# A four-layer image network on one core: one more product on GpSimd, another order of the last image's scans, and bias work on VectorE at the end

## The chip, the core and the metric

The kernel runs on one core of a Trainium2 chip. The core has TensorE (PE in the profile), VectorE (DVE), ScalarE (ACT), GpSimd (POOL) and SyncE (SP, which here issues every DMA). The metric is the device time of one execution in microseconds; the kernel before was run three times.

## What is computed

Four images of 96 channels and 64 x 64 pixels pass through four layers. What matters here is the first, a selective scan in four directions, and the feed-forward blocks of the last two, which round to 8-bit and 16-bit floats:

```python
# layer 0: K, N, DI = 4 orders, 16 states, 192 channels; L = 4096 pixels
xs = jnp.stack([xf, xt, jnp.flip(xf, -1), jnp.flip(xt, -1)], axis=1)   # rows, columns, and both backwards
...
dA = jnp.exp(dt_[..., None] * A[None])
hst = hst * dA + (dt_ * ut)[..., None] * bt[:, :, None, :]
y = jnp.einsum('bkdn,bkn->bkd', hst, ct)
...
y = y0 + y1 + y2 + y3            # orders 1 and 3 turned back to rows
# then a norm over channels, a product with Wout, and the residual

def _qlinear(x, W, b):           # in the feed-forwards of layers 2 and 3
    y = q_acc(jnp.einsum('bsk,nk->bsn', q_mul(x), q_mul(W)))
    return q_acc(y + q_mul(b))
h = jax.nn.relu(_qlinear(x, W1, b1))
y = _qlinear(h, W2, b2)
```

Layer 1 is an expansion to 576 channels, a 3 x 3 depthwise convolution and a projection; layer 2 starts with a Fourier transform over the pixels, layer 3 with a linear attention. Each has its own residual.

## The kernel before

**The scan is the backbone.** `scans` builds a list of 128 *steps*: for each image, for each order k in `KORDER` = (0, 1, 3, 2), for each of 8 chunks of 512 pixels. Orders 0 and 2 go over rows, 1 and 3 over columns; 2 and 3 run backwards, so their chunks come from 7 down to 0. A step has 12 *units*, one for each pair of 32-channel groups and quarter of the states: units 0 to 7 are the first pass (128 channels), 8 to 11 the second (64). A loop over *slots* writes the program out by hand, one unit a slot, each engine's part at its own offset:

- ScalarE, one slot ahead (`decays`): first `keep`, which saves the last column of an earlier unit as the start of the next chunk, then two exponentials of 128 x 512 into PSUM (line 1188).
- GpSimd, two slots ahead (`inputs`): db = g * B, one product of 128 x 1024 (line 1178).
- VectorE (`states`): two scans of 128 x 512 (line 1197), and for most units two products with C (line 1201).
- For units whose number is in `POOL_C` = (1, 3, 6, 8, 10), GpSimd multiplies with C instead, a slot later (`product`, line 1216, 128 x 1024), and also saves the last columns (line 1213; otherwise ScalarE does, line 1211).
- TensorE adds the states of two units into a PSUM tile (`sums`, line 1237), two slots after the later one. After the last pair of a pass ScalarE copies the tile out (line 1245) and two stores of y are put down with `later`.

g, the step widths and B, C are tiles broadcast from DRAM. `LOADS` says at which unit a tile of the next step is loaded: B and C of state quarter 0 at unit 4, quarter 1 at unit 10, quarter 2 at unit 11, quarter 3 at unit 0 of the step itself. Five buffers hold the B, C tiles (rep_BC), three the others. `later` only notes a store; `flush`, the first thing in a slot, issues what was noted. All loads and stores stand in SP's one queue.

**The work beside.** Everything else is written as Python generators that yield the engine, a guessed cost and the PSUM banks of their next piece. In each slot `advance` takes pieces from the first *stage* in a list while the slot's room lasts. `SHARE` gives an engine's room: (us added per slot, most that is kept), 3.0 and 3.2 for TensorE, 2.4 and 3.0 for ScalarE, 1.2 and 1.7 for VectorE. The stages in order: weights, `front` of images 1 and 2 (input convolution and the scans' inputs), for image 0 the turn, layer 1 with the scan's output stage (`conv_block`), layers 2 and 3, then `front` of image 3, and images 1 and 2 likewise. The layer 1 stage of the last image comes at the end of the list.

**The turn** (`turn`) adds orders 1 and 3, turned by strided reads, to order 0 and the skip term, in two parts: channels 0 to 127 (lo = 0) and the other 64 (lo = 128). A part loads 2 x 2 MB of y (lines 636 to 638 are its matmuls). It waits until three orders of its image are scanned (`scanned[b] < 3 * NCH`); those of images 2 and 3 stand in one stage with layer 3 of the image before. `scan_outputs` then adds order 2, chunk by chunk (line 677), as soon as its last order has passed a chunk, and the output norm follows (lines 696 to 713).

**The tail.** After the last slot, what is left is issued by `force`, without regard to slots, and with all eight PSUM banks (`alone` is not empty then): the rest of layer 1 of image 3 (lines 763, 786, 802, 803, and 839, 845 of its norms), the two halves of the Fourier layer, layer 2's end and layer 3, three chunks at a time. In `feed_forward` each of three 128-row parts of the hidden layer takes three passes of ScalarE: a copy from PSUM to 16 bits (line 868), bias and relu (line 871), rounding to 8 bits (line 873).

Of the kernel before, what the change touches and what calls it, by code (L numbers as in the profile page):

```python
# [37 lines left out]
NI, NJ = DI // 32, NS // 4  # L38
ROWB = 256

KORDER = (0, 1, 3, 2)

SCAN = {"rep_d": 3, "rep_g": 3, "rep_BC": 5, "db": 3, "hc": 5}
POOL_C = (1, 3, 6, 8, 10)
TMP, IN = 10, 5

PC = NI * NJ // 2
# [4 lines left out]
WORK = {"weights": 47.0, "turn": 70.0, "front": 417.0, "conv": 447.0,  # L52
        "spectral": 111.2, "layer_2": 231.0, "product": 1.2, "layer_3": 153.6, "layer_3_turn": 223.6}
RATE = 6.0
SHARE = {"pe": (3.0, 3.2), "act": (2.4, 3.0), "dve": (1.2, 1.7)}
NQ, NG, NPAIR = 4, HID // 32, H // 2


# [35 lines left out]
def hybrid_kernel(ctx: ExitStack, tc: tile.TileContext, a: dict):  # L94
# [45 lines left out]
    def const(name, rows=slice(0, 128)):  # L140
        return cst[rows, CS[name]]
# [282 lines left out]

    to_store = []

    def later(out, t):

        to_store.append((out, t))

    def flush():
        while to_store:
            store(*to_store.pop(0))

    def ahead(n, first, items):

# [3 lines left out]
                got.append(first(items[len(got)]))  # L440
            yield item, got[i]

    def in_turn(items, make, matmuls, take, evict, depth=2):

        made = []

        def oldest():
            p, item, at = made.pop(0)
            yield take[:3] + (at,)
            evict(p, item)  # L450
            free()

        for n, item in enumerate(items):
            yield make[:3] + (n > 0,)
            p = bank()
            matmuls(p, item)
            made.append((p, item, clock[0]))
            if len(made) == depth:
                yield from oldest()
        while made:  # L460
            yield from oldest()
# [147 lines left out]

    def turn(b):  # L610

        im = b % 2
        while scanned[b] < 3 * NCH:
            yield wait(1)
        parts = [big("ya"), big("yb")]
        for lo in (0, 128):
            for t, k in zip(parts, (1, 3)):
                load(t[:, :L].rearrange("p (c l) -> p c l", c=NCH),
                     d_y[k][im][:, lo : lo + 128, :].rearrange("c p l -> p c l"))

            def fetch(c):
                y, u = (t[:, L + c % 4 * CH : L + c % 4 * CH + CH] for t in parts)
                load(y, d_y[0][im][c, lo : lo + 128])
                load(u[: min(128, DI - lo)], d_skip[b][c, lo : min(lo + 128, DI)])
                return y, u

            whole = lo == 0
            m, add = (128, const("ident")) if whole else (64, const("two")[:, :64])
            skip = skips[:, 0] if whole else skips[:64, 1, :64]

            def added(p, of):
                c, (y, u) = of
# [4 lines left out]
                mm(p, lhsT=add, rhs=y, start=False, stop=False)  # L637
# [10 lines left out]
            yield from in_turn(chain([first], chunks), pe(3.8, 1), added, ac(0.6), stored)  # L648
            yield wait(2)

    def scan_outputs(b, done):

        there = lambda c: scanned[b] >= 4 * NCH - c

        def fetch(c):
            out = []
            for of in (d_yt[b % 2][c], d_y[2][b % 2][c]):
                for part in (of[:128], of[128:]):
                    s = arrival("ypart")
                    load(s[: part.shape[0]], part)  # L660
                    out.append(s[: part.shape[0]])
            return out[0], out[2], out[1], out[3]

        coming = None
        for c in reversed(range(NCH)):
            while not there(c):
                yield wait(1)
            if coming is None:
                coming = fetch(c)
                yield wait(3)  # L670
            parts, coming = coming, None
            y = []
            for name, of in (("ident", parts[:2]), ("two", parts[2:])):
                yield pe(1.8, 1, name == "two")
                p = bank()
                for n, s in enumerate(of):
                    mm(p, lhsT=const(name, slice(0, s.shape[0])), rhs=s, start=n == 0, stop=n == 1)  # L677
# [178 lines left out]
    def feed_forward(x, weights):  # L856

        wq1, wq2, bq = weights
        xq = tmp("xq", (128, CH), F8)
        yield from layer_norm(x[:C], xq)  # L860
        hq = tmp("hq", (128, 3, CH), F8)
        for m in range(3):
            yield pe(0.5, 1, m > 0)
            p = bank()
            mm(p, lhsT=wq1[:, m * 128 : (m + 1) * 128], rhs=xq, start=True, stop=True)
            yield ac(0.65)
            acc = tmp("acc16", (128, CH), F16)
# [252 lines left out]
    def scans(stages):  # L1120
# [6 lines left out]

        steps = []
        for b in range(B):
            for k in KORDER:  # L1130
# [95 lines left out]
        def sums(group):  # L1226
# [6 lines left out]
            for m in (1, 0):  # L1233
                x = group[m]
                for e in (1, 0):
                    q = 2 * m + e
                    done = mm(y[32 * q : 32 * q + 32], lhsT=const("stack"), rhs=x["hc"][:, e],  # L1237
                              start=first or (x["pass"] == 0 and x["j"] == 0), stop=last or (x["pass"] == 0 and x["j"] == NJ - 1))
                    if made is None:
                        made = group[0]["made"]  # L1240
                        tc.add_manual_dep(done.ins, made.ins.name, mybir.DependencyInfo(
                            mybir.DependencyClass.Sync, mybir.DependencyReason.DATA), reason="sums")
            if last:
# [299 lines left out]
```

## Time and profile before

| | us |
|---|---|
| three runs | 6702.1, 6703.26, 6710.55 (median 6703.26) |
| the profiled execution | 6708.94 |
| its span, first to last instruction | 6707.1 |
| first scan starts, last scan ends (line 1197) | 78.8, 6125.9 |
| layer 1 of image 3, last block ends | 6323 |
| the Fourier layer ends | 6472 |
| layer 2 ends, layer 3 begins | 6605 |

| engine | busy us | share | instructions |
|---|---|---|---|
| TensorE, matmuls | 4836.7 | 72% | 27884 |
| VectorE | 5521.4 | 82% | 5803 |
| ScalarE | 4357.4 | 65% | 8296 |
| GpSimd | 5173.5 | 77% | 2743 |

The profile's page gives busy times, the span in 40 slices, the chain of work that ended last, and the costliest groups of instructions: line, engine, operation, output<-inputs, shape, count | busy us, mean ns of one | idle time of the engine just before them and what ended most of it. The trace also answers for a stretch of time: busy time of each engine in it, the clock that TensorE was granted, and the share of the DMA engines' time. A float32 matmul of the program is two records. Busy times of neighbouring instructions can overlap by some tens of ns, so that sums of means lie a little above busy time.

### The profile page before, as it was taken

Reading aid. Unit: us, or ns where it says so; the run is one execution under the profiler, and the core shown is the slowest. Engines: PE = TensorE matmul, PEld = TensorE weight load, DVE = VectorE, ACT = ScalarE, POOL = GpSimd, SP = SyncE. Lnnn points to the kernel's source line nnn. Section 1 sums busy time; section 2 is a strip of 40 time slices with the busy share of each in tenths; the row PEclk is TensorE's granted clock in tenths of the full one; section 3 lists DMA queues with packets and bytes.
Section 4 is the critical chain, followed back from the end, with each engine's and each line's share of the span. In section 5 each row is a group of like instructions: output and inputs, shape, how many; then the busy total and the mean of one; then the engine's idle time right before and its main releaser. Section 6 shows DMA issues by size and latency. Waiting matters only on the chain. (4 is left out here: it accounts for less than half of the span.)

```text
span 6707.1 us, 84452 instructions
## 1 busy us (share of the span) xinstructions
PE 4836.7 (72%) x27884; PEld 1777.4 (26%) x27884; DVE 5521.4 (82%) x5803; ACT 4357.4 (65%) x8296; POOL 5173.5 (77%) x2743
## 2 busy tenths in 40 slices
PE   7633857657987676775688777777887776779986
PEld 2100212111223531121122254221223532213562
DVE  5979899898999889889999988887999889895110
ACT  5743767765665577876556656866665677755367
POOL 4756878789999789977999988888999889894000
PEclk9755968768998787797799988878998887889997
DMA  5644555576644544455765454465644544563120
GB/s 185 193 157 142 180 188 188 180 239 231 188 152 143 181 154 145 156 187 187 257 208 165 147 168 167 144 208 176 193 151 151 193 157 145 202 230 101 38 82 27
DMA packets 438825, 1121.42 MB, mean 167 GB/s; under 512 B 73002, under 2 KB 74768, under 8 KB 437140
## 3 DMA queue, kind: packets, MB, share of 16 engines
q1 hardware_dynamic: 438388, 1116.02, 50.9%
q8 instruction: 222, 3.64, 0.2%
q14 instruction: 215, 1.76, 0.1%
HBM read 881.28 MB, written 239.01 MB: 167 GB/s over the span
## 5 line engine op out<-in xcount | busy, mean ns | idle before, releaser
L1178 POOL TENSOR_TENSOR db<-rep_g,rep_BC 128x1024 f32<-128x1024 f32 x1536 | 3600.2, 2364 | 551.0 <-DMA rep_BC<-bc 281.9
L1188 ACT ACTIVATE ps_da<-rep_d,aneg 128x512 f32<-128x512 f32 x3072 | 2067.3, 690 | 542.0 <-DVE hc L1197 404.5
L1197 DVE TENSOR_TENSOR_SCAN ps_da<-ps_da,state,db 128x512 f32<-128x512 f32 x1568 | 2007.1, 1280 | 237.3 <-ACT state L1211 154.5
L1216 POOL TENSOR_TENSOR hc<-hc,rep_BC 128x1024 f32<-128x1024 f32 x640 | 1510.8, 2361 | 91.0 <-DVE hc L1197 41.4
L1237 PE MATMUL ps_y<-hc,cst 128*32 128x512 f32 x6144 | 1026.7, 746 | 619.3 <-POOL hc L1216 348.2
L1197 DVE TENSOR_TENSOR_SCAN hc<-ps_da,state,db 128x512 f32<-128x512 f32 x1120 | 1371.1, 1266 | 70.3 <-ACT ps_da L1188 23.1
L1201 DVE TENSOR_TENSOR hc<-ps_da,rep_BC 128x512 f32<-128x512 f32 x1792 | 1239.2, 692 | 112.5 <-PE ps_y L1237 3.9
L1211 ACT COPY state<-ps_da 128x1 f32<-128x1 f32 x1568 | 247.2, 158 | 471.1 <-DVE hc L1201 466.3
L1237 PEld LDWEIGHTS ps_y<-hc,cst 128*32 128x32 f32 x6144 | 145.8, 119 | 1264.8 <-POOL hc L1216 556.6
L786 PE MATMUL ps_mm<-h,wd 128*32 128x512 f32 x3048 | 348.5, 593 | 7.0 <-ACT r L153 7.0
L1213 POOL COPY state<-hc 128x2 f32<-128x2 f32 x560 | 106.0, 189 | 306.9 <-DVE hc L1197 294.2
L531 PE MATMUL ps_mm<-xp,taps 128*128 128x512 f32 x576 | 293.6, 652 | 41.5 <-ACT xp L511 14.4
L1197 DVE TENSOR_TENSOR_SCAN ps_da<-ps_da,db 128x512 f32<-128x512 f32 x224 | 273.6, 1221 | 41.7 <-ACT state L1211 23.8
L582 PE MATMUL ps_mm<-xd,dtw 128*128 128x512 f32 x256 | 177.1, 783 | 162.2 <-ACT z L604 116.2
L763 PE MATMUL ps_mm<-wd,w 128*32 128x512 f32 x2032 | 261.2, 621 | 36.8 <-DMA wd<-x 11.9
L1245 ACT COPY yt<-ps_y 128x512 f32<-128x512 f32 x256 | 149.1, 582 | 151.1 <-PE ps_y L1237 145.1
L591 ACT ACTIVATE z<-ps_mm 128x512 f32<-128x512 f32 x192 | 114.3, 595 | 167.8 <-PE ps_mm L582 106.6
L912 PE MATMUL ps_mm<-wa,xp 128*64 128x96 f32 x1728 | 143.2, 327 | 103.1 <-DVE d L916 79.1
L597 DVE SCALAR_TENSOR_TENSOR ps_mm<-ps_mm,z 128x512 f32<-128x512 f32 x192 | 132.3, 689 | 99.1 <-ACT z L595 69.6
L1197 DVE TENSOR_TENSOR_SCAN hc<-ps_da,db 128x512 f32<-128x512 f32 x160 | 186.2, 1204 | 9.4 <-ACT ps_da L1188 9.0
L845 PE MATMUL ps_mm<-r,cst 128*128 128x512 f32 x206 | 138.8, 761 | 70.8 <-ACT acc L868 26.6
L569 PE MATMUL ps_mm<-ua,sel 128*128 128x512 f32 x128 | 101.3, 880 | 114.7 <-ACT z L604 91.1
(420 smaller groups left out, 6954.1 us busy)
## 6 DMA issues: line engine op xcount, KB each, us to landing
rep_BC<-bc SPq DMA_DIRECT2D x512, 512.0 KB
rep_g<-du SPq DMA_DIRECT2D x384, 512.0 KB
rep_d<-delta SPq DMA_DIRECT2D x384, 512.0 KB
y<-yt SPq DMA_DIRECT2D x512, 128.0 KB
du<-g SPq DMA_DIRECT2D x128, 256.0 KB
delta<-z SPq DMA_DIRECT2D x128, 256.0 KB
tab<-in_etab SPq DMA_DIRECT2D x128, 256.0 KB
du<-g SPq DMA_DIRECT2D x128, 128.0 KB
```

Of the source, the lines that this page charges most:

```text
L531: mm(p, lhsT=taps[:, t, 0:128], rhs=window(t, c + e), start=t == 0, stop=t == 8)
L582: mm(p, lhsT=dtw[:, o + 2 * part, 0:128], rhs=xd, start=True, stop=True)
L763: mm(p[32 * n : 32 * n + 32], lhsT=w1[:, 32 * g : 32 * g + 32], rhs=xin[:, n : n + 15 : 2, 1 : W + 1], start=True, stop=True)
L786: mm(p[32 * n : 32 * n + 32], lhsT=held["wd"][:, groups[i], o, dx, :], rhs=here[i][:, :, dx : dx + W], start=dx == 0, stop=dx == 2)
L1178: nc.gpsimd.tensor_mul(x["db"], x["step"]["g"][x["i"]], both(x["step"]["BC"][x["j"]][:, 0]))
L1188: act(x["da"][e], x["step"]["d"][x["i"]][:, e], AF.Exp, scale=aneg[:, av : av + 1])
L1197: nc.vector.tensor_tensor_scan(x["h"][e][:, order], x["da"][e][:, order], x["db"][:, e, order], start, ALU.mult, ALU.add)
L1201: x["made"] = nc.vector.tensor_mul(x["hc"][:, e], x["h"][e], x["step"]["BC"][x["j"]][:, 1])
L1211: nc.scalar.copy(to[:, e : e + 1], x["h"][e][:, end : end + 1])
L1216: x["made"] = nc.gpsimd.tensor_mul(x["hc"], x["hc"], both(x["step"]["BC"][x["j"]][:, 1]))
L1237: done = mm(y[32 * q : 32 * q + 32], lhsT=const("stack"), rhs=x["hc"][:, e], start=first or (x["pass"] == 0 and x["j"] == 0), stop=last or ...
L1245: nc.scalar.copy(yt, y)
```

## The change

Three things change, and some numbers of the planner with them.

1. `POOL_C` becomes (1, 3, 5, 7, 9, 11): six of twelve units have their C product on GpSimd, every second one. `SHARE` becomes 2.4 and 2.8 for ScalarE and 1.5 and 2.0 for VectorE.
2. The last image's orders are scanned as 1, 3, 0, 2. Its turn may start when two orders are through; the part with lo = 128 comes first and leaves y0 out, the part with lo = 0 takes y0's chunks as order 0's scan delivers them (`ready`). `scan_outputs` of the last image loads y0's upper rows as a fifth piece and adds them there. The turn goes over its chunks upwards instead of downwards, for all images. `scanned` counts a chunk when its second store is issued, no longer when it is noted. `flush` moves behind the slot's loads of B, C, g and step widths.
3. When nothing but the tail is left (`alone`), `feed_forward` does bias and relu on VectorE, and for the middle of the three parts the rounding to 8 bits too.

```diff
-KORDER = (0, 1, 3, 2)
+KORDER = [(0, 1, 3, 2)] * (B - 1) + [(1, 3, 0, 2)]
-POOL_C = (1, 3, 6, 8, 10)
+POOL_C = (1, 3, 5, 7, 9, 11)
-SHARE = {"pe": (3.0, 3.2), "act": (2.4, 3.0), "dve": (1.2, 1.7)}
+SHARE = {"pe": (3.0, 3.2), "act": (2.4, 2.8), "dve": (1.5, 2.0)}
...
     def flush():
         while to_store:
-            store(*to_store.pop(0))
+            out, t, then = to_store.pop(0)
+            store(out, t)
+            if then is not None:
+                then()
...
-        for n, item in enumerate(items):
+        items, n = iter(items), 0
+        while True:
+            while ready is not None and not ready(n):
+                yield wait(1)
+            item = next(items, None)
+            if item is None:
+                break
             yield make[:3] + (n > 0,)
...
-        while scanned[b] < 3 * NCH:
+        early = b == B - 1
+        while scanned[b] < (2 if early else 3) * NCH:
             yield wait(1)
-        for lo in (0, 128):
+        for lo in (128, 0) if early else (0, 128):
+            rows = not (early and lo == 128)
...
-                load(y, d_y[0][im][c, lo : lo + 128])
+                if rows:
+                    load(y, d_y[0][im][c, lo : lo + 128])
...
-            chunks = ahead(1, fetch, reversed(range(NCH)))
-            first = next(chunks)
+            chunks = ahead(1, fetch, range(NCH))
+            ready = (lambda n: scanned[b] >= 2 * NCH + min(n + 2, NCH)) if early and rows else (lambda n: True)
...
+            yt, y0, y2 = (of[b % 2][c] for of in (d_yt, d_y[0], d_y[2]))
+            for part in (yt[:128], y2[:128], yt[128:], y2[128:]) + ((y0[128:],) if b == B - 1 else ()):
...
-            yield ac(0.65)
-            act(acc, acc, AF.Relu, bias=bq[:, m : m + 1])
-            yield ac(0.65)
-            nc.scalar.activation(hq[:, m, :], acc, AF.Copy, saturate=False)
+            if alone:
+                yield dv(0.75)
+                nc.vector.tensor_scalar(acc, acc, bq[:, m : m + 1], 0.0, ALU.add, ALU.max)
+            else:
+                yield ac(0.65)
+                act(acc, acc, AF.Relu, bias=bq[:, m : m + 1])
+            if alone and m == 1:
+                yield dv(0.75)
+                nc.vector.tensor_copy(hq[:, m, :], acc, saturate=False)
+            else:
+                yield ac(0.65)
+                nc.scalar.activation(hq[:, m, :], acc, AF.Copy, saturate=False)
...
-                    later(to[at : at + 64].rearrange("(p e) l -> e p l", e=2), yt[64 * m : 64 * m + 64])
-                if group[0]["pass"] == 1:
-                    scanned[step["b"]] += 1
+                    later(to[at : at + 64].rearrange("(p e) l -> e p l", e=2), yt[64 * m : 64 * m + 64],
+                          through if group[0]["pass"] == 1 and m == 1 else None)
...
-            flush()
             if x is not None:
                 if x["u"] == 0:
...
                     fetch(steps[x["number"] + 1], LOADS[x["u"]])
+            flush()
             if slot + 1 < len(units):
                 decays(units[slot + 1], units[slot - 1] if slot > 0 else None)
```

More of the change, by code (lines that the diff above doesn't have):

```diff
@@ L425, in hybrid_kernel, with later @@
     to_store = []
-    def later(out, t):
-        to_store.append((out, t))
+    def later(out, t, then=None):
+        to_store.append((out, t, then))
     def flush():
         while to_store:
-            store(*to_store.pop(0))
+            out, t, then = to_store.pop(0)
+            store(out, t)
+            if then is not None:
+                then()
     def ahead(n, first, items):
@@ L441, in ahead, with in_turn @@
             yield item, got[i]
-    def in_turn(items, make, matmuls, take, evict, depth=2):
+    def in_turn(items, make, matmuls, take, evict, depth=2, ready=None):
         made = []
@@ L457, in in_turn @@
             made.append((p, item, clock[0]))
+            n += 1
             if len(made) == depth:
@@ L636, in added @@
                     mm(split(p), lhsT=add, rhs=rhs, start=n == 0, stop=False)
-                mm(p, lhsT=add, rhs=y, start=False, stop=False)
+                if rows:
+                    mm(p, lhsT=add, rhs=y, start=False, stop=False)
                 mm(p, lhsT=skip, rhs=u[: skip.shape[0]], start=False, stop=True)
@@ L643, in stored @@
                 later(d_yt[im][of[0]][lo : lo + m], s)
-            chunks = ahead(1, fetch, reversed(range(NCH)))
-            first = next(chunks)
+            chunks = ahead(1, fetch, range(NCH))
+            ready = (lambda n: scanned[b] >= 2 * NCH + min(n + 2, NCH)) if early and rows else (lambda n: True)
             yield wait(10)
-            yield from in_turn(chain([first], chunks), pe(3.8, 1), added, ac(0.6), stored)
+            yield from in_turn(chunks, pe(3.8, 1), added, ac(0.6), stored, ready=ready)
             yield wait(2)
@@ L656, in fetch @@
             out = []
[L657 to L662, printed above, removed]
+            yt, y0, y2 = (of[b % 2][c] for of in (d_yt, d_y[0], d_y[2]))
+            for part in (yt[:128], y2[:128], yt[128:], y2[128:]) + ((y0[128:],) if b == B - 1 else ()):
+                s = arrival("ypart")
+                load(s[: part.shape[0]], part)
+                out.append(s[: part.shape[0]])
+            return out
         coming = None
@@ L676, in scan_outputs @@
                 for n, s in enumerate(of):
-                    mm(p, lhsT=const(name, slice(0, s.shape[0])), rhs=s, start=n == 0, stop=n == 1)
+                    mm(p, lhsT=const(name, slice(0, s.shape[0])), rhs=s, start=n == 0, stop=n == len(of) - 1)
                 yield ac(0.6)
@@ L1129, in scans @@
         for b in range(B):
-            for k in KORDER:
+            for k in KORDER[b]:
                 for n in range(NCH):
@@ L1242, in sums, with through @@
                             mybir.DependencyClass.Sync, mybir.DependencyReason.DATA), reason="sums")
+            def through():
+                scanned[step["b"]] += 1
             if last:
```

## The prediction

> **What bounds the kernel now.** I read the page's engine line first, then the costliest groups.
>
> ```profile
> PE 4836.7 (72%) x27884; PEld 1777.4 (26%) x27884; DVE 5521.4 (82%) x5803; ACT 4357.4 (65%) x8296; POOL 5173.5 (77%) x2743
> ...
> L1178 POOL TENSOR_TENSOR db<-rep_g,rep_BC 128x1024 f32<-128x1024 f32 x1536 | 3600.2, 2364 | 551.0 <-DMA rep_BC<-bc 281.9
> ...
> L1201 DVE TENSOR_TENSOR hc<-ps_da,rep_BC 128x512 f32<-128x512 f32 x1792 | 1239.2, 692 | 112.5 <-PE ps_y L1237 3.9
> ...
> L1213 POOL COPY state<-hc 128x2 f32<-128x2 f32 x560 | 106.0, 189 | 306.9 <-DVE hc L1197 294.2
> ```
>
> Nothing is full on average, so the average decides nothing. The instructions of the scan (line 1197) run from 78.8 to 6125.9 us; behind them lies a tail of 581 us without GpSimd. I cut the scan part at every 24th scan into its 128 steps (one chunk of one order of one image; mean 47.2 us) and took busy time by windows. These are four windows of typical steps (3 to 5; 46 to 49; 100 to 103; the turn of image 2, steps 90 to 93), then the turn of image 3 (120 to 123), then the four parts of the tail. Columns: stretch, length, busy PE, PEld, DVE, ACT, POOL, clock, DMA.
>
> ```profile
> 236.70:398.80 162.10, 94.08 (x248) 20.18 (x252) 156.68 (x169) 118.21 (x236) 121.93 (x66) 0.70 0.62 197
> 2382.30:2571.20 188.90, 131.78 (x497) 44.99 (x498) 161.77 (x171) 146.93 (x281) 162.02 (x85) 0.81 0.46 151
> 4887.50:5052.10 164.60, 141.18 (x994) 38.90 (x994) 159.29 (x166) 110.70 (x217) 161.62 (x84) 0.94 0.45 153
> 4413.80:4632.10 218.30, 171.48 (x438) 43.56 (x439) 159.37 (x161) 140.27 (x281) 164.48 (x90) 0.87 0.59 193
> 5777.60:5954.60 177.00, 136.38 (x356) 30.89 (x356) 154.66 (x157) 105.04 (x216) 162.53 (x89) 0.85 0.69 241
> ...
> 6125.00:6323.00 198.00, 189.48 (x1264) 70.45 (x1256) 14.08 (x26) 72.32 (x113) 0.00 (x0) 0.98 0.12 33
> 6323.00:6472.00 149.00, 136.70 (x2565) 133.41 (x2565) 29.52 (x38) 81.36 (x99) 0.00 (x0) 0.95 0.33 102
> 6472.00:6605.00 133.00, 96.61 (x341) 42.18 (x341) 12.13 (x22) 92.82 (x165) 0.00 (x0) 0.83 0.12 36
> 6605.00:6707.00 102.00, 65.44 (x175) 24.86 (x171) 6.58 (x13) 73.84 (x131) 0.00 (x0) 0.79 0.07 22
> ```
>
> The reader is to see three kinds of step. Steps 3 to 5: VectorE 97%, GpSimd 75%. Steps 46 to 49: both at 86%, ScalarE with much work beside. Steps 100 to 103: VectorE 97% and GpSimd 98%, both at the limit. In the tail, TensorE is 96% busy in the rest of the convolution, and ScalarE 70% and 72% in the two last parts. Last, GpSimd's waits (the releaser, us in total, times, longest):
>
> ```profile
> POOL state L1213 <- DVE hc L1197: 294.2, 202, 38.8
> POOL db L1178 <- DMA rep_BC<-bc: 281.9, 84, 11.0
> ```
>
> [...]
>
> **Part 1: six of twelve products on GpSimd.** Per step GpSimd has 12 x 2.364 + 5 x 2.361 + 4.4 copies x 0.189 = 41.0 us; after, 12 x 2.364 + 6 x 2.361 + 5.25 x 0.189 = 43.5, each about 0.3 less since neighbours overlap. (Line 1216, the C product, has a mean of 2361 ns in the page.) VectorE loses 2 x 0.692 = 1.4 per step, ScalarE 224 state copies (line 1211, 158 ns each) = 35 us in all. I sorted the steps by the work that the built order of instructions puts between their scans, at this trace's mean duration for each line: "VectorE-heavy" (over 45 us of VectorE work), "ScalarE-heavy" (of the others, over 38 of ScalarE), "light" (rest).
> - Before: 37 at 54.6, 30 at 47.3, 61 at 42.8 us measured: 6047 us.
> - VectorE-heavy after: the new order has 36, with 1.0 us less VectorE work each (the planner, whose VectorE share is now 1.5 a slot instead of 1.2, packs beside-work denser): 53.6.
> - ScalarE-heavy after: 29. GpSimd has some 6 us of idle time in such a step, which takes the 2.5. VectorE's 1.4 less counts in part, since it waits there for exponentials; nine of the 30 are below 44.3 today and will not stay there. I take 47.0 (ends 46.0 and 48.5).
> - Light after: 63. Here the bound is GpSimd: 43.2 and what it waits. It waits 2.8 per light step now, 1.55 of it for rep_BC. I take 1.0, so 44.2 (ends 43.5: no waits, 46: all of them).
> Sum 36 x 53.6 + 29 x 47.0 + 63 x 44.2 = 6078: **+31 us**.
>
> Why waits should shrink: SP is one queue, and stores were flushed ahead of a slot's loads. At 1790.0 two y stores, which had waited for their copy out of PSUM, stand before the load of the second BC tile, whose db product then starts 1.7 us late (1800.5). After, a slot's four loads go first. And that tile's buffer was held by unit 8's product on GpSimd, a slot later than by VectorE, which has unit 8 now. In heavy steps this is hidden; VectorE waits for db only 59 us in all. I count **-10**. The stores stand behind at most four issues of 0.55 us; their readers are stages later, so nothing. If that cover fails, one slot (3.4 us) at the end.
>
> **Part 2: orders 1, 3, 0, 2 for the last image and its early turn.** The inputs of all orders are made by step 62, image 3 starts at 96: nothing. The eight matmuls of y0's upper rows leave the turn and come back in the output stage with a fifth load of 256 KB per chunk: same count, nothing. The turn moves from steps 120-123, where its 8 MB of loads cost almost nothing (177.0 us; by class means 47.3+3x42.8 = 176), to 116-119, beside the last feed-forwards of image 2, where image 2's own turn cost 218.3 against 180. In the new order 116-119 hold as much ScalarE and TensorE work as 90-93 did. But its second half lies in light steps. Between 0 and +38 I take **+20**.
>
> What it frees: the convolution of the last image starts about four steps earlier. In the built order, matmuls after the last scan fall from 324 to 240 (line 786), 216 to 148 (763), 40 to 30 (802, 803), 64 to 60 (839, 845). Prices from the chain (a float32 matmul is two records):
>
> ```profile
> 6089.80 2.58 PE ps_mm L786 x24
> ...
> 6092.38 2.61 PE ps_mm L763 x24
> ...
> 6194.38 3.60 PE ps_mm L802 x8
> ```
>
> 84 x 0.215 + 68 x 0.217 + 10 x 0.9 + 4 x 0.86 = 45, and one wait of 4.9 for a block's input (in the chain, DMA wd<-x at 6263.0): **-50**, since TensorE is 96% busy there. Inside the scans TensorE has room (72%). Ends -35, -60.
>
> **Part 3: VectorE in the last feed-forwards.** ScalarE loses 48 bias-and-relu at 0.67 net (32.3 us in the tail) and a third of 27.2 for hq: 41 us. It is busy 71% of these stretches, TensorE's start of each group of three chunks holds the rest, so I take 0.7 x 41 = **-28**. New wait: ScalarE's hq behind VectorE's relu; queued behind it are the next copies out of PSUM. A group keeps 9 x 0.59 + 6 x 0.56 = 8.7 us on ScalarE and gets 12 VectorE operations[...]. Ends -10 (each handoff stalls) and -40.
>
> Sum against the profiled execution (span 6707.1, time 6708.9): 6708.9 + 31 - 10 + 20 - 50 - 28 = 6672. That execution is 5.7 above the median of the runs: **6666**.
>
> **Rivals.**
> - *More gain*: GpSimd hardly waits (43.5) and ScalarE-heavy steps fall with VectorE (46.3): 63 x 0.7 = 44 and 29 x 0.7 = 20 less: 6602. For it: VectorE's longest waits are on ScalarE, which is relieved. Against: 84 waits of GpSimd on DMA will not all go.
> - *Slower*: GpSimd becomes the bound of all light steps and keeps its waits, 45.4 us each: +76, so about 6742. Its place is steps 25-38, 63-75, 94-103 and 120-127; it decides from 44.8 us per light step, where the tail's gain is used up. For it: light steps have no slack on GpSimd. Against: in steps 100-103 GpSimd ran at 98% with waits of only 0.8 a step.
> - *Part 3 does nothing* (handoffs cost what ScalarE saves): 6694.
>
> **How the numbers follow.** Forecast 0.49, with a range of its own of 6630 to 6693; more gain 0.18; slower 0.26; part 3 nothing 0.07. A measurement of this kernel can tell about 0.2% (13 us) from no change. Faster (below 6690): 0.46 + 0.18 = 0.64; within: 0.12; slower (over 6716): 0.24. The range leaves out the lower half of "more gain" and the upper third of "slower": 6600 to 6745.
>
> **What would show it.** Light steps near 44.2 us with GpSimd at 98%; the rep_BC wait well below 282 us; last scan near 6167; a tail of about 503 us instead of 581, its convolution part about 148 instead of 198; ScalarE in the two last parts under 130 us. Wrong if light steps pass 44.8, if steps 116-119 take over 218, or if the last parts stay at 235.

## The result: no difference

Twelve runs of the kernel after have a median of 6703.1 us (6693.0 to 6709.5), twelve of the kernel before beside them 6706.4 (6702.1 to 6710.6). The ratio is 0.9996 with a 95% interval of 0.9987 to 1.0005. The forecast was 6666, the chance given to "within 0.2%" was 0.12. The profiled execution has a span of 6707.7.

First the engine line of the page after, and the groups of db, of VectorE's C product and of GpSimd's saved columns (lines 1206, 1229, 1241 now):

```profile
PE 4872.1 (73%) x27884; PEld 1775.4 (26%) x27884; DVE 5391.2 (80%) x5611; ACT 4269.2 (64%) x8008; POOL 5488.7 (82%) x2983
...
L1206 POOL TENSOR_TENSOR db<-rep_g,rep_BC 128x1024 f32<-128x1024 f32 x1536 | 3602.0, 2365 | 194.1 <-DVE ps_da L1225 115.0
...
L1229 DVE TENSOR_TENSOR hc<-ps_da,rep_BC 128x512 f32<-128x512 f32 x1536 | 1062.3, 692 | 91.3 <-DVE ps_da L1225 1.3
...
L1241 POOL COPY state<-hc 128x2 f32<-128x2 f32 x672 | 128.4, 191 | 395.3 <-DVE hc L1225 374.1
```

The work moved as counted: GpSimd has 240 instructions and 315 us more, VectorE 130 us less, ScalarE 88 us less. The idle time ahead of db fell from 551 to 194 us, and B and C no longer head its releasers. Now the windows, in the order of those of before (steps 3 to 5, 46 to 49, 100 to 103, the turn of image 2, the turn of image 3 in its new place at 116 to 119, then the four parts of the tail):

```profile
231.50:395.10 163.60, 95.13 (x246) 20.15 (x246) 155.54 (x165) 119.53 (x235) 129.83 (x73) 0.70 0.65 207
2433.10:2603.50 170.40, 118.25 (x495) 38.98 (x493) 155.90 (x165) 140.86 (x271) 167.77 (x90) 0.86 0.47 154
4935.70:5107.80 172.10, 142.28 (x973) 37.34 (x972) 155.33 (x157) 111.83 (x211) 170.58 (x92) 0.93 0.44 148
4491.90:4676.90 185.00, 140.79 (x380) 32.63 (x379) 153.59 (x154) 125.86 (x252) 167.62 (x95) 0.83 0.60 202
5663.70:5856.90 193.20, 155.10 (x413) 36.66 (x406) 154.23 (x153) 142.64 (x272) 168.42 (x90) 0.88 0.55 186
6207.00:6368.00 161.00, 149.10 (x952) 55.09 (x944) 10.30 (x19) 52.95 (x83) 2.37 (x1) 0.95 0.12 36
6368.00:6512.00 144.00, 132.99 (x2565) 129.37 (x2564) 29.38 (x38) 81.95 (x100) 0.00 (x0) 0.99 0.34 104
6512.00:6632.00 120.00, 99.93 (x374) 45.66 (x374) 22.65 (x57) 75.59 (x137) 0.00 (x0) 0.89 0.14 42
6632.00:6708.00 76.00, 58.21 (x140) 21.15 (x140) 15.98 (x43) 53.70 (x96) 0.00 (x0) 0.89 0.10 29
```

Read the last four first. The tail is 499.8 us long (6207.9 to 6707.7), 81 less than before. The scans end 82 us later, at 6207.9. So the gain at the end came as forecast, and all of it was lost among the scans. Sorted by the classes of the prediction (work between two scans, of each kernel's own trace for the kernel after), the scan part reads:

| class | before: steps, mean us | forecast | after |
|---|---|---|---|
| light | 61, 42.8 | 44.2 | 62, 44.1 |
| ScalarE-heavy | 30, 47.3 | 47.0 | 30, 46.0 |
| VectorE-heavy | 37, 54.6 | 53.6 | 36, 55.8 |

Light steps match, ScalarE-heavy ones are better, and the VectorE-heavy ones became some 1.3 us longer although each has 0.9 us less VectorE work. Against the forecast of 53.6 that is some 80 us over 36 steps. They lie mostly in the *fronts* (input convolution and inputs of the scans): steps 8 to 23 took 853 us before and 892 after, which is half of the 82.

### The profile page after: what moved, and what is told of

Same layout as the page of the kernel before. It is cut to its first block, busy times and chain, and to the rows that moved or that the text cites. A ratio compares the mean times of both kernels' runs of the same rounds, so it can differ in the third digit from the quotient of the medians.

```text
span 6707.7 us, 84354 instructions
## 1 busy us (share of the span) xinstructions
PE 4872.1 (73%) x27884; PEld 1775.4 (26%) x27884; DVE 5391.2 (80%) x5611; ACT 4269.2 (64%) x8008; POOL 5488.7 (82%) x2983
## 5 line engine op out<-in xcount | busy, mean ns | idle before, releaser
L1206 POOL TENSOR_TENSOR db<-rep_g,rep_BC 128x1024 f32<-128x1024 f32 x1536 | 3602.0, 2365 | 194.1 <-DVE ps_da L1225 115.0
L1216 ACT ACTIVATE ps_da<-rep_d,aneg 128x512 f32<-128x512 f32 x3072 | 2053.5, 689 | 499.4 <-DVE hc L1225 381.7
L1225 DVE TENSOR_TENSOR_SCAN ps_da<-ps_da,state,db 128x512 f32<-128x512 f32 x1344 | 1722.9, 1282 | 371.8 <-ACT state L1239 226.7
L1244 POOL TENSOR_TENSOR hc<-hc,rep_BC 128x1024 f32<-128x1024 f32 x768 | 1813.4, 2361 | 131.8 <-DVE hc L1225 64.8
L1225 DVE TENSOR_TENSOR_SCAN hc<-ps_da,state,db 128x512 f32<-128x512 f32 x1344 | 1645.8, 1266 | 173.0 <-ACT ps_da L1216 155.9
L1229 DVE TENSOR_TENSOR hc<-ps_da,rep_BC 128x512 f32<-128x512 f32 x1536 | 1062.3, 692 | 91.3 <-DVE ps_da L1225 1.3
L1241 POOL COPY state<-hc 128x2 f32<-128x2 f32 x672 | 128.4, 191 | 395.3 <-DVE hc L1225 374.1
L1239 ACT COPY state<-ps_da 128x1 f32<-128x1 f32 x1344 | 212.8, 158 | 343.9 <-DVE hc L1229 343.0
L805 PE MATMUL ps_mm<-h,wd 128*32 128x512 f32 x3192 | 365.7, 593 | 7.7 <-ACT r L154 7.0
L1225 DVE TENSOR_TENSOR_SCAN ps_da<-ps_da,db 128x512 f32<-128x512 f32 x192 | 234.6, 1222 | 56.9 <-ACT state L1239 36.0
L1225 DVE TENSOR_TENSOR_SCAN hc<-ps_da,db 128x512 f32<-128x512 f32 x192 | 223.4, 1204 | 17.3 <-ACT ps_da L1216 13.2
L609 DVE SCALAR_TENSOR_TENSOR ps_mm<-ps_mm,z 128x512 f32<-128x512 f32 x192 | 131.9, 687 | 84.0 <-ACT z L607 56.4
L786 ACT ACTIVATE h<-ps_mm 128x512 f32<-128x512 f32 x266 | 153.9, 596 | 44.6 <-PE ps_mm L782 42.5
```

The source lines that it names most:

```text
L786: act(h[:, :, 1 : W + 1], split(p), AF.Relu)
L805: mm(p[32 * n : 32 * n + 32], lhsT=held["wd"][:, groups[i], o, dx, :], rhs=here[i][:, :, dx : dx + W], start=dx == 0, stop=dx == 2)
L1206: nc.gpsimd.tensor_mul(x["db"], x["step"]["g"][x["i"]], both(x["step"]["BC"][x["j"]][:, 0]))
L1216: act(x["da"][e], x["step"]["d"][x["i"]][:, e], AF.Exp, scale=aneg[:, av : av + 1])
L1225: nc.vector.tensor_tensor_scan(x["h"][e][:, order], x["da"][e][:, order], x["db"][:, e, order], start, ALU.mult, ALU.add)
L1229: x["made"] = nc.vector.tensor_mul(x["hc"][:, e], x["h"][e], x["step"]["BC"][x["j"]][:, 1])
```

## The experiments

Each ratio below has an interval of about +/-0.13%, so a difference of two versions is known to some 12 us. The versions were measured in four batches, each beside the kernel before. Its medians there were 6701.9 us (e1 to e4), 6699.9 (e5 to e8), 6700.7 (e9 to e12) and 6706.9 (e13 to e16), and 6706.4 beside the kernel after. A difference of medians across batches can therefore be off by a few us more. Where two versions come from different batches, the difference of their ratios to the kernel before is given in brackets, in us. Stretches and tails are those of one profiled execution each; those of e5, e6, e15 and e16 were 10 to 13 us below the median of their version. Line numbers of versions with the first-load edit are two higher.

**Which part lengthens the scans?** Two suspects: A, the planner's new room packs the fronts more densely; B, each pair's sum now waits for a GpSimd product of the *later* unit, and matmuls queue behind it (TensorE's waits for that product grew from 557 us at weight loads and 348 at matmuls to 1096 and 760; the two kinds of record can count the same time).

```diff
 # e1_old_share, from the kernel after
-SHARE = {"pe": (3.0, 3.2), "act": (2.4, 2.8), "dve": (1.5, 2.0)}
+SHARE = {"pe": (3.0, 3.2), "act": (2.4, 3.0), "dve": (1.2, 1.7)}
 # e2_old_pool, from the kernel after
-POOL_C = (1, 3, 5, 7, 9, 11)
+POOL_C = (1, 3, 6, 8, 10)
 # e3_old_both: both edits
 # e4_first_of_pair, from the kernel after
-POOL_C = (1, 3, 5, 7, 9, 11)
+POOL_C = (0, 2, 4, 6, 8, 10)
```

> Six products on GpSimd as in the kernel after, but the planner's room as before (2.4 and 3.0 for ScalarE, 1.2 and 1.7 for VectorE). The steps with much VectorE work beside them took 55.9 us each in the kernel after, where 53.6 had been forecast: 36 x 2.3 = 81 us. Theory A (packing): the new room puts more pieces of the input projections into one slot, so that TensorE, ScalarE and VectorE hand pieces to and fro within a slot and the exponentials come late. Then these steps fall to about 53.6 and the time to about 6622. Theory B (late product): each pair's sum now waits for a GpSimd product of the pair's later unit, and the matmuls queued behind it wait too. Then nothing changes here: VectorE-heavy steps near 55.9, time near 6703.

Measured 6671.6 us, 31.5 less than after (30), between the two expectations. VectorE-heavy steps: 53.9, as theory A has it; scan part 6078 us instead of 6129, tail 515 instead of 500.

> The other half: five products on GpSimd as before (units 1, 3, 6, 8, 10), the room of the kernel after. By both theories the light steps fall from 44.15 back to about 42.8 us, 63 x 1.35 = 85 us. Theory A (packing): the VectorE-heavy steps keep their trouble and get 1.4 us of VectorE work more, 36 x up to 1.4 = up to 50; time about 6650 to 6670. Theory B (late product): they go back to 54.6 or below, as only two of six pairs then end on a late product: 36 x 1.3 = 45 less; with 29 ScalarE-heavy steps up to 1 us longer, the time is about 6600 to 6625.

Measured 6710.7: no gain, and 54 us more than e3 below, which differs in the room alone. Light steps fell only to 43.4, and VectorE-heavy ones rose to 56.4.

> Five products on GpSimd and the room as before: only the new order of the last image with its early turn, the moved stores and the VectorE work at the end are left of the change. By both theories the scan part is nearly that of the kernel before (6047 us), plus up to 20 for the turn beside layer 3 and less up to 10 for stores behind loads, and the tail is the 500 us of the kernel after instead of 581: about 6706 - 81 + 10 = 6635, between 6620 and 6650. If it stays above 6690, the loss lies in the early turn or in the moved stores, and neither theory holds.

Measured 6656.8 (ratio 0.9931, 0.9919 to 0.9944), 22 above the expectation. Its light steps are 43.5, not 42.8.

> Six products on GpSimd, but those of the first unit of each pair (0, 2, 4, 6, 8, 10), so that a sum waits for a product a slot older; the load on every engine is that of the kernel after. Light steps stay at about 44.2 by both theories. Theory A (packing): VectorE-heavy steps stay near 55.9, time 6695 to 6710. Theory B (late product): TensorE's waits for GpSimd's product, 1856 us over both kinds of record in the kernel after, fall to less than half, VectorE-heavy steps go to about 53.6, and the time to about 6622.

Measured 6739.8, 37 more than after (37). The sums of TensorE with the idle time before them and what ended most of it, first of the kernel after, then of e4:

```profile
L1265 PE MATMUL ps_y<-hc,cst 128*32 128x512 f32 x6144 | 1037.4, 755 | 781.5 <-POOL hc L1244 759.5 <-ACT ps_da L1216 10.8 <-DVE bq L419 5.4
...
L1265 PEld LDWEIGHTS ps_y<-hc,cst 128*32 128x32 f32 x6144 | 141.7, 119 | 1450.8 <-POOL hc L1244 1096.0 <-issue 243.4 <-POOL db L1206 61.8
```

```profile
L1265 PE MATMUL ps_y<-hc,cst 128*32 128x512 f32 x6144 | 1018.5, 741 | 569.8 <-DVE hc L1229 283.3 <-POOL hc L1244 266.1 <-ACT ps_da L1216 8.5
...
L1265 PEld LDWEIGHTS ps_y<-hc,cst 128*32 128x32 f32 x6144 | 146.9, 118 | 1225.4 <-issue 554.6 <-POOL hc L1244 474.5 <-POOL db L1206 156.6
```

The waits put down to GpSimd's product fell as expected, to 741 us from 1856. But much of that idle time only changed its name: all idle time ahead of the sums fell from 2232 to 1795 us. No step got shorter for it (VectorE-heavy 56.1, ScalarE-heavy 46.5, light 44.4). B's forecast fails: these waits are the largest in the list, and a good part of them can go without a gain. Why e4 is slower still was not settled, and that loss could hide a small gain. A holds for the VectorE-heavy steps of e1, but e2 is 41 us over the upper end of A's range and 86 over B's, and e3 showed that something else had made light steps longer.

**A load that lost its head start.** Against the kernel before, e3 lost 17 us each in steps 24 to 31 and 64 to 71, where turns begin. In e3 TensorE's weight loads wait 60 us in all for `DMA ya<-y`, in the kernel before 2.1. The diff explains it: `first = next(chunks)` ahead of `yield wait(10)` is gone, so that a turn's first chunks of y and of the skip term are loaded only when its first matmul is issued. In the kernel before that load was issued 24 us ahead of the turn's first matmul:

```profile
1465.08 4.41 SPq L623 DMA_DIRECT2D ya<-y  x1
...
1488.77 0.50 PEld L636 LDWEIGHTS ps_mm<-ya,cst 128*128 128x128 f32 x2 [1.66 <-issue]
```

The chain of the kernel after at the first turn, cut from the timeline (start, us, engine, line; in brackets the idle time before it and what ended it):

```profile
1478.21 0.58 SPq L640 DMA_DIRECT2D ya<-y  x1
...
1488.70 0.50 PEld L655 LDWEIGHTS ps_mm<-ya,cst 128*128 128x128 f32 x2 [8.30 <-DMA ya<-y]
...
1492.42 0.20 PEld L1265 LDWEIGHTS ps_y<-hc,cst 128*32 128x32 f32 x8 [1.50 <-issue]
...
1493.80 0.59 ACT L1276 COPY yt<-ps_y 128x512 f32<-128x512 f32 x1 [10.26 <-PE ps_y L1265]
...
1494.76 1.32 ACT L1216 ACTIVATE ps_da<-rep_d,aneg 128x512 f32<-128x512 f32 x2
...
1495.56 2.46 DVE L1225 TENSOR_TENSOR_SCAN hc<-ps_da,state,db 128x512 f32<-128x512 f32 x2 [5.75 <-ACT ps_da L1216]
```

The load is issued at 1478.2, the matmul that needs it (L655) starts 10.5 us later. The scan's sum stands behind that matmul, ScalarE's copy of the sum behind the sum, the next exponentials behind the copy, and VectorE's scan waits 5.75 us for them. No instruction of VectorE uses this load. The same place with the load ahead (e6):

```profile
1442.85 5.31 SPq L640 DMA_DIRECT2D ya<-y  x1
...
1470.33 0.50 PEld L653 LDWEIGHTS ps_mm<-ya,cst 128*128 128x128 f32 x2 [1.66 <-issue]
...
1473.08 0.21 PEld L655 LDWEIGHTS ps_mm<-ya,cst 128*128 128x128 f32 x1 [0.65 <-issue]
```

```diff
 # e5_first_load_old_both, from e3; e6_first_load, from the kernel after
+            if not (early and rows):
+                chunks = chain([next(chunks)], chunks)
             yield wait(10)
             yield from in_turn(chunks, pe(3.8, 1), added, ac(0.6), stored, ready=ready)
```

> The version with five products on GpSimd and the room as before (6656.8 us), and one thing more undone: the turn again loads its first chunks of y and of the skip term before it waits its ten slots, instead of at the first matmul (left as it is where the last image's y0 is still being scanned). The changed kernels have waits of TensorE for this load at the start of each part of a turn, 10 to 12 us each for images 0 and 1 in the version with both undone, and the kernel before has none; steps 24 to 31 and 64 to 71 were 17 us longer each than before. Theory C (late first load): these waits vanish, those two stretches go back to about 355 and 345 us, and the time to about 6622. Rival (the stores behind the loads, or the upward order of the chunks, make these steps longer): no change, 6650 to 6660.

> The kernel after with this one line back: first chunks of a turn loaded before its wait. In the kernel after TensorE waits for these loads 8.3, 8.6, 2.6, 3.7, 7.0, 7.8 and 2.1 us at the parts of the turns, 40 us in all. Theory C (late first load): some 10 to 35 us less than 6703, most likely 20, as the stall of TensorE reaches VectorE only in part. Rival: within 5 us of 6703.

Measured 6616.3 for e5 (ratio 0.9882, 0.9867 to 0.9897), 40 less than e3 (33); steps 24 to 31 take 347 us instead of 372, steps 64 to 71 338 instead of 362, and no other group of eight steps changed by 5 us or more. So the loss lay where the late loads were. Measured 6667.5 for e6, 36 less than the kernel after (26). Theory C holds, at the upper end of what was expected: the waits of TensorE in the kernel after are 40 us in all, and most of that reached the end.

**VectorE's room alone, and the tail alone.**

```diff
 # e7_vector_share, from the kernel after
-SHARE = {"pe": (3.0, 3.2), "act": (2.4, 2.8), "dve": (1.5, 2.0)}
+SHARE = {"pe": (3.0, 3.2), "act": (2.4, 2.8), "dve": (1.2, 1.7)}
 # e8_scalar_tail_old_both, from e3, in feed_forward
-            if alone:
+            if False:
...
-            if alone and m == 1:
+            if False:
```

> The kernel after with VectorE's room alone as before (1.2 a slot, 1.7 at most), ScalarE's at 2.4 and 2.8. With both as before the time was 6671.6. If VectorE's room does the harm by letting more pieces of the input projections into a slot, the time is 6665 to 6680 and VectorE-heavy steps take about 54 us; if ScalarE's lower cap (2.8 for 3.0) does it, the time stays at 6695 to 6705 and those steps near 55.9.

Measured 6668.4, as in e1: VectorE's room does the harm, ScalarE's cap none that shows.

> The version with five products on GpSimd and the room as before (6656.8 us), with bias, relu and rounding at the end on ScalarE as before: it prices part 3 alone. The prediction has 28 us for it, between 10 and 40: then 6685, all of it behind the last scan. If the handoffs to VectorE cost what ScalarE saves, 6657.

Measured 6694.1, 37 more than e3 (41), all of it behind the last scan (tail 552 instead of 515). Two windows, layer 2 behind the Fourier layer and layer 3 behind its attention sums (what lies between is left out), first of e8, then of e3:

```profile
6446.00:6552.50 106.50, 81.53 (x307) 36.92 (x306) 9.38 (x18) 72.46 (x130) 0.00 (x0) 0.84 0.14 41
6584.70:6686.60 101.90, 64.31 (x141) 23.09 (x140) 6.33 (x12) 72.62 (x128) 0.00 (x0) 0.76 0.07 22
```

```profile
6446.00:6538.70 92.70, 79.83 (x305) 36.61 (x304) 16.85 (x42) 58.26 (x106) 0.00 (x0) 0.91 0.16 47
6567.10:6649.50 82.40, 60.64 (x140) 22.42 (x140) 16.33 (x44) 53.98 (x96) 0.00 (x0) 0.86 0.09 27
```

With VectorE's help (e3) ScalarE has 14.2 and 18.6 us less work, and the stretches are 13.8 and 19.5 us shorter. Each us taken off ScalarE shortened them by about one, although it is busy only 68% and 71% of them in e8, and the new waits cost nothing that shows.

**The other terms, each taken out of e5.**

```diff
 # e9_stores_first, from e5: flush() again first in the slot
             x = units[slot] if slot < len(units) else None
+            flush()
...
-            flush()
             if slot + 1 < len(units):
 # e10_old_order, from e5
-KORDER = [(0, 1, 3, 2)] * (B - 1) + [(1, 3, 0, 2)]
+KORDER = [(0, 1, 3, 2)] * B
...
-        early = b == B - 1
+        early = False
...
-            for part in (yt[:128], y2[:128], yt[128:], y2[128:]) + ((y0[128:],) if b == B - 1 else ()):
+            for part in (yt[:128], y2[:128], yt[128:], y2[128:]) + ():
 # e11_six, from e5
-POOL_C = (1, 3, 6, 8, 10)
+POOL_C = (1, 3, 5, 7, 9, 11)
```

> The version with the first load of a turn, five products and the old room (6616.3 us), with the noted stores issued first in a slot again, ahead of its loads. The prediction has 10 us for the move: GpSimd's db products waited 282 us for B and C in the kernel before and hardly wait after. Then 6626, and these waits are back at over 200 us. Rival (they hide in VectorE-heavy steps): 6616 within 5.

Measured 6658.8: 42 more than e5 (35), about four times the forecast and far from the rival. GpSimd's waits for B and C, e9 first, e5 second:

```profile
POOL db L1208 <- DMA rep_BC<-bc: 251.2, 81, 9.8
```

```profile
POOL db L1208 <- DMA rep_BC<-bc: 22.1, 10, 5.0
```

From e9 to e5 light steps go from 43.1 to 42.7 (25 us in all), and ScalarE-heavy ones from 47.3 to 46.3 (31 us), which I had given nothing. The two sum to more than 42 because the profiled execution of e5 lies 13 us below that version's median. Both have five products, so the order of issue alone removes these waits; that unit 8's product no longer holds a buffer of B and C, the prediction's second reason, was not needed. e9 also answers a rival that no run took out alone, the upward order of the turn's chunks and the later count in `scanned`: both are in e9, and its steps 0 to 111 take 5327 us, those of the kernel before 5334.

> The same version (6616.3 us) with the last image's orders as before, 0, 1, 3, 2, and its turn after three of them. The prediction has 50 us of gain for the convolution that leaves the end, and 20 of loss for the turn beside layer 3: then 6646, with the tail longer by 50 and the scan part shorter by 20. In the version with five products and the old room steps 112 to 127 took no longer than those of the kernel before plus 15, so a rival is: the early turn costs nothing, and the time is 6660 to 6670.

Measured 6621.1, below both expectations: 5 more than e5 by the medians, 5 less by the ratios, so no difference. By the profiled executions the tail is 32 us longer and the scan part 15 shorter. e5 and e10 are the fastest versions of this study.

> The same version (6616.3 us) with six of twelve products on GpSimd: part 1 without the planner's room. The prediction has 31 us for it, light steps near 44.2 instead of 42.7 and 1.4 us less VectorE work in the VectorE-heavy ones: 6647. With the turn's loads late, six instead of five gave 6671.6 against 6656.8, 15 more: the rival, 6631, has VectorE's and ScalarE's relief pay half of what GpSimd's light steps cost.

Measured 6645.3 (ratio 0.9913, 0.9898 to 0.9929), 29 more than e5 (21). Light steps 43.8, VectorE-heavy 53.9.

**What the room does.** e11 and e6 differ in the room alone. Their steps 8 to 23 take 835.6 us and 889.6 us; the window of each (columns as above) and its waits:

```profile
539.70:1375.30 835.60, 537.92 (x1704) 150.59 (x1704) 746.90 (x793) 573.80 (x1066) 691.81 (x373) 0.78 0.57 187
```

```profile
ACT z L603 <- PE ps_mm L594: 50.2, 33, 3.1
...
PE ps_mm L598 <- ACT z L616: 38.2, 14, 5.5
...
DVE ps_da L1227 <- ACT state L1241: 24.8, 15, 4.0
```

```profile
539.70:1429.30 889.60, 571.77 (x1732) 157.34 (x1732) 760.16 (x806) 596.56 (x1101) 689.56 (x372) 0.77 0.54 178
```

```profile
ACT z L603 <- PE ps_mm L594: 63.3, 38, 5.0
...
DVE ps_da L1227 <- ACT state L1241: 56.6, 21, 7.9
...
PE ps_mm L598 <- ACT z L616: 54.9, 22, 4.1
```

The dense version gets 13 us more VectorE work and 23 us more ScalarE work into these steps, and pays 54 us of time. A matmul of the projection (594, 598) waits until ScalarE's copy z (616) has emptied a PSUM tile, ScalarE's next pass (603) waits for the matmul, the saved columns and exponentials stand behind it in ScalarE's queue, and VectorE's scans wait. That would be the same coupling as in the late load; here it is read from the waits that grew and from the order of the program, not shown by a run of its own.

```diff
 # e12_front_room, from the kernel after; e14_front_room_five, from e5 with the new SHARE
             for e, (us, most) in SHARE.items():
+                if e == "dve" and stages and stages[0].name == "front":
+                    us, most = 1.2, 1.7
 # e13_less_room, from e5
-SHARE = {"pe": (3.0, 3.2), "act": (2.4, 3.0), "dve": (1.2, 1.7)}
+SHARE = {"pe": (3.0, 3.2), "act": (2.4, 3.0), "dve": (1.0, 1.5)}
 # e15_room_five, from e5: the SHARE of the kernel after
 # e16_old_order_room_six, from e6: the three edits of e10
```

> The kernel after (6703), where VectorE's room is held at the old 1.2 and 1.7 only while a front stage (input convolution and the scans' inputs) is first in the planner's list. Steps 8 to 23 took 892 us in the kernel after and 838 with the old room throughout. If the harm lies in fronts packed too densely, these steps go back to about 840, the tail stays near 500, and the time is 6640 to 6660. If it lies in the room anywhere, no more than 10 to 15 us are gained.

Measured 6684.8, 18 less than after (13), where 6640 to 6660 had been expected of fronts as the only place. Steps 8 to 23 went back to 846 us as expected, but less came of it than they had lost: later steps became longer, and the tail 512 us.

> The version with the first load of a turn, five products and the old room (6616.3 us), with less room for VectorE: 1.0 a slot and 1.5 at most instead of 1.2 and 1.7. If a denser packing of the work beside the scans is what costs time, less room shortens the scan part further (6005 us) by 10 to 30 and leaves 10 to 30 more for the tail (517): 6600 to 6630. If 1.2 is at its best, the tail gets more than the scan part gives: over 6630.

Measured 6753.6, a miss: the scan part is only 8 us shorter and the tail 161 longer. With 1.0 a slot much of the work beside the scans no longer fits among them.

> The same version (6616.3 us) with the new room (2.8 for ScalarE's cap, 1.5 and 2.0 for VectorE), save that VectorE keeps 1.2 and 1.7 while a front stage is first in the list. With six products and late loads this hold won back 18 of the 35 us that VectorE's room costs. If half the harm of the room lies in the fronts, this takes 6625 to 6635; if the rest of the room pays when the fronts are spared, 6600 to 6612, with a tail near 505.

Measured 6649.0, a miss as well, 33 more than e5 (23): sparing the fronts isn't enough. Most of the loss shows in steps 104 to 111, which hold a Fourier layer: 390 us instead of 353. Waits in these steps, e14 first, then e5:

```profile
ACT f L990 <- PE ps_mm L986: 28.5, 10, 9.1
...
PE ps_mm L986 <- DMA tab<-in_etab: 23.2, 7, 9.5
...
DVE ps_da L1227 <- ACT ps_da L1218: 15.1, 4, 7.4
DVE hc L1227 <- ACT ps_da L1218: 11.2, 2, 9.7
```

```profile
ACT f L990 <- PE ps_mm L986: 9.3, 9, 1.9
...
PE ps_mm L986 <- DMA tab<-in_etab: 5.4, 4, 2.7
...
DVE hc L1227 <- ACT ps_da L1218: 2.5, 2, 1.3
```

It seems that with more room the layer reaches its tables before their loads have landed, and that the wait travels TensorE, ScalarE's copy, exponentials, scan, as in the turn. No run tested this by itself.

> The same version (6616.3 us) with the new room alone. With six products and late loads the room cost 31 us, with six products and early loads 22, with five products and late loads 54. If five products leave VectorE fuller, so that packing more beside it costs more, the time is 6650 to 6665; if the 54 came from the late loads, 6635 to 6642.

Measured 6674.9, above both expectations: with five products the room costs 59 us (46) with the early loads and 54 with the late ones (e3 to e2); with six it costs 22 (29) and 31 (30). VectorE-heavy steps take 56.4 us with five and 55.7 with six.

> The kernel after with the first load of a turn back (6667.5 us), with the last image's orders and turn as before. With five products and the old room the new order gave only 5 us by the medians (6621.1 to 6616.3), where 30 had been forecast. If the new order pays only with the new room, which moves more of the last convolution into the scans, this takes 6690 to 6700; if it is worth little in any setting, 6665 to 6678.

Measured 6685.9, 18 more than e6 (7), between the two expectations. With the new order the tail goes from 542 to 496 and the scan part from 6051 to 6081. In both settings the order shortens the tail and lengthens the scans, and a net gain isn't shown in either: by the ratios it is 7 us here and -5 with the old room.

## Why the prediction was wrong, point by point

| term of the sum | forecast | measured, medians | by the ratios | from, to |
|---|---|---|---|---|
| stores behind loads (the SP waits) | -10 | -42 | -35 | e9 to e5 |
| VectorE in the last feed-forwards | -28 | -37 | -41 | e8 to e3 |
| new order, early turn, old room | -50 + 20 | -5 | +5 | e10 to e5 |
| new order, early turn, new room | -50 + 20 | -18 | -7 | e16 to e6 |
| six of twelve products | +31, room included | +29 | +21 | e5 to e11 |
| the planner's room | inside the +31 | +22 | +29 | e11 to e6 |
| first load of a turn | not costed | +36 | +26 | e6 to after |

The last three are steps of one path, from e5 to the kernel after. The first three were each measured by themselves; added up with the old room they are -84 (by the ratios -71), where e5 lies 84 (79) below the kernel before, so little is left for parts not listed. Two edits, the order of stores and loads and VectorE's work at the end, had made some 80 us; the sixth product, the room and the late load took it back. That the sum came out at nothing is chance: every part but the new order moved the time.

- **The step that failed outright**: part 2 listed what the turn issues and where it moves, but its working is silent on the removed `first = next(chunks)`. It stood in the diff. The trace of before shows those loads on SP 24 us ahead of the first matmul (1465.1 and 1488.8). The prediction charged image 3's turn with contention and left the three other turns, which only lost their head start, at nothing. This costs 26 to 40 us.
- **The term with the wrong size**: "VectorE-heavy 53.6". With the old room it is right (53.9 in e1 and e11). I had counted the planner's VectorE share of 1.5 as work that moves. With it the steps took 55.7 to 55.8 (e6, after); the waits (those of VectorE's scans into `ps_da` for ScalarE's saved columns, in steps 8 to 23, are 24.8 us in e11 and 56.6 in e6) suggest that dependent pieces of TensorE, ScalarE and VectorE come closer together and hold up the exponentials. Net of the shorter tail, the room costs 22 to 31 us, and part 1 as the forecast had it, room included, +51 instead of +31.
- **The other wrong size**: the new order, -30 forecast. It shortened the tail by 32 to 46 us instead of 50 and lengthened the scan part by 15 to 30 instead of 20, so that no net gain is shown.
- **Right in sum, by parts that made up for each other**: the tail, -78 forecast and -81 found. Its convolution part gained 37 us instead of 50, the last two parts 39 instead of 28 (196 instead of 235, ScalarE in them 129.3 us), and the Fourier part 5. Some 15 of the 81 come with the new room, since with the old room the tail is 515 (e1, e3, e11); the forecast counted matmuls in the built order of the whole new kernel and put all of that down to the new order of the scans. Light steps at 44.1 agree with 44.2 partly by accident, since the late loads are in them: 43.5 without (e6).
- **Right in kind, wrong in size**: stores behind loads. I had priced the waits of light steps only; ScalarE-heavy steps gained more. The turn beside layer 3: steps 116 to 119 took 193 us, below the bound of 218, and 112 to 127 together take 31 more than with the old order (726 in e6, 695 in e16), for 20 forecast.
- **What the moved operations took**: the forecast left GpSimd's products at their means of before, and with 256 C products fewer on VectorE they stayed there: db 2364 ns before and 2365 after, the C product 2361 in both (L1216 before, L1244 after). For VectorE's new operations of the tail the trace of before has no row; that twelve of them fit beside ScalarE's 8.7 us of a group was my estimate. Measured are 348 ns for bias and relu and 422 ns for the rounding to 8 bits, where ScalarE takes 623 (L901 in the tail), so the twelve of a group take about 9 x 0.348 + 3 x 0.422 = 4.4 us:

```profile
L892 DVE TENSOR_SCALAR acc<-acc,bq 128x512 f16<-128x512 f16 x48 | 15.6, 348 | 13.3 <-ACT acc L887 13.3
...
L898 DVE CAST hq<-acc 128x512 fp8e5<-128x512 f16 x16 | 6.4, 422 | 0.3
```

- None of the three signs that were to show the forecast wrong came (light steps over 44.8, steps 116 to 119 over 218, last parts at 235). They watched the terms I had doubted, and the loss lay in two that I had not.
- **Open**: why the room costs more with five products (46 to 59) than with six (22 to 31), which was only seen to lie in the VectorE-heavy steps; by what chain of waits the room costs time at all; and the slowness of e4.

## What to carry to other kernels

Read a diff for loads that lose their head start as carefully as for operations that are added: here a matmul that waited 8.3 us for a load held back the scan's sum, ScalarE's copy of it, the exponentials behind the copy and at last VectorE, and the list of waits put VectorE's part down to the exponentials. Price a planner's budget by an experiment of its own, since more room does more than move work: here it cost 22 to 59 us. When a change with several parts moves the time by nothing, take the parts out one at a time: here the version with three of them and the early load (e5) is 1.2% faster than the kernel before, and 1.1% faster than the kernel after.

## What was not expected of the hardware

A wait of TensorE for one 256 KB load of y, 8.3 us long, reached VectorE's scan as a wait of 5.75 us, and taking such waits away (40 us in all) gave 26 to 36. In e4 TensorE was idle 437 us less ahead of its sums, and no step got shorter. The size of an entry in the list of waits said little about its price here. In the one chain that was followed, the wait passed on because ScalarE had a copy of a TensorE result queued ahead of the exponentials; that this decides in general was not tested.
